# Layer 0's sums and layer 1's transposes moved from TensorE to VectorE and DRAM, and tiles of exponentials turned through DRAM with a fourth buffer

## The chip, the cores and the metric

The kernel runs on one NeuronCore of a Trainium2 chip. The metric is device time in microseconds of one execution. A profile is one more execution, recorded by the chip; in its rows PE is TensorE (PEld its weight loads), DVE is VectorE, ACT is ScalarE, POOL is GpSimd, SP is SyncE, which issues all DMAs here (SPq is its queue).

## The reference

Input x has 4 images of 128 channels by 64x64 pixels, so N = 4096 positions. In short:

```
# layer 0
g    = group_norm(x)                                    # 32 groups of channels
v,gt = split(sigmoid(conv_bn(g, Wvg)))                  # 1x1 convolutions
attn = softmax(q k^T / 8), q, k of 64 channels from g
x    = x + conv_bn(v attn^T * gt, Wp)
# layer 1, on tokens t = x^T, per image
h    = layer_norm(t)
q    = h W
t    = t + softmax(q q^T) h                             # q is also the key: symmetric
h2   = layer_norm(t)
wx   = batch_norm(h2 Wffn^T)                            # statistics over all tokens
y_i  = sigmoid(wx_i + y_(i-1) V^T)                      # recurrence along tokens
out  = (t + y)^T
```

All is float32. The softmax of a query divides the weighted sum of values by the sum of its exponentials. That sum (the denominator) and the transposes between "channels by positions" and "tokens by channels" are what the change is about.

## The kernel before, in words

`fast` (line 143) holds the whole of the work; `general` is another path that isn't run with these data. For each of four images (batches, b) `layer0` and then `layer1` are issued, both in blocks of 512 queries (n = 0..7). A block has four tiles of 128 positions (j). The remaining work of a block, once its attention is complete, is cut into small functions ("items") that are put in the list `pending`; the preparation of the next batch (norm, projections, gates) stands in the list `ahead`. The loops take one item from these lists at each step, so that their instructions stand between the big matmuls.

**Layer 0** (`attention`, line 178): 16 steps p per block. A step has two score matmuls (`ps`, line 200; 64 rows each, the two share the array), one exponential of 128x1024 on ScalarE (`e`, line 202), one VectorE add of the exponentials into `acc` (lines 207, 209), and, two steps later, four weighting matmuls into `o` (line 383). When a block is complete (`finish`, line 389) six items follow: `sums` (403) calls `denominators` (222), which adds the halves of `acc` and lets TensorE sum over the 128 partitions with four matmuls against a column of ones (`md`, line 227), and moves the input block `xb` to tokens; `projection` (407; `mt`, line 409) moves its result to tokens; `tokens` (412) adds the two and norms; `queries` (422; `mq`, line 424) makes `qt` of the moved layer norm `ht`.

**move** (line 235) is a transposition of 128x512 without TensorE: VectorE transposes 32x32 blocks into `d` (line 241), SP writes `d` to a DRAM tile `turn_d` (256 KB, line 244), waits for it, and reads it back in four parts in the other order (line 246).

**Layer 1** (`layer1`, line 435): since queries are keys, the scores are symmetric, and only the pairs of blocks (n, a) with a <= n are computed, in the order n = 6, 7, 5, ..., 0 and a = n, ..., 0. Each pair is two steps i. A step has two score matmuls (`ps`, line 562), two exponentials of 128x512 with their sums in `slots` (`e`, line 568), and two weighting matmuls later (`o`, line 455). For a < n VectorE also transposes the exponentials in blocks of 32x32 into `dd` (line 573, two buffers), and when a pair is complete 16 DMAs of 64 KB (line 594) carry `dd` to its turned place in `tt` (three buffers). Four steps later `reversed_products` (463) uses the turned tile for block a: four matmuls (`ot`, line 468), the sums of the tile into `slots` (line 473), and the sum of `ot` into `oacc` (`part`, lines 482 and 484).

A block n is complete after eight such parts; `finish` (495) loads its tokens `t` from DRAM and appends four items: `tokens` (504) sums the slots, transposes `oacc` on TensorE (`mt`, line 511), adds to the tokens (513) and norms into `h2`; `result` (520) transposes the tokens back on TensorE (`mr`, 523), copies them on ScalarE and stores them; `turn` (528) transposes `h2` on TensorE (`mh`, 531) and copies it to `th` on ScalarE (532); `inputs` (534) multiplies `th` (`mw`, 536) and stores the result for the recurrence. `layernorm` (250) works on VectorE, with two small instructions on GpSimd (lines 116, 117) in between.

The PSUM tiles `m` of all these items share one bank; the scores `ps` have two buffers, the exponentials `e` four. At the end the recurrence runs from line 640 on.

The instructions of an engine run in the order in which they stand in the built program. That is not quite the order of the code: when the program is built, an instruction is put where the builder expects its inputs to be ready, and later ones may go ahead of it. So `mw` may stand behind matmuls that the code has after it. SP's DMAs are one such order too.

Of the kernel before, what the change touches and what calls it, by code (L numbers as in the profile page):

```python
# [10 lines left out]
F32 = mybir.dt.float32  # L11
# [38 lines left out]
def conv_attn_hybrid_kernel(  # L50
# [14 lines left out]
    wxs_d = dram.tile([B, P, L // 2, G, 2], F32, name="wxs_d")  # L65
    t_d = dram.tile([B, NB, P, 4, NQ, 32], F32, name="t_d")

    turn_d = [dram.tile([P, 4, NQ, 32], F32, name=f"turn{i}_d") for i in range(8)]
    t2_d = dram.tile([B, C, N], F32, name="t2_d")
    wx_d = dram.tile([B, C, N], F32, name="wx_d")  # L70
# [43 lines left out]
    def inv_sqrt(dst, var, eps):  # L114
# [3 lines left out]

    par_ok = const.tile([P, 4], F32, name="par_ok")
    fast(  # L120
        tc, x, out, t_d, t2_d, wxs_d, turn_d,
        dict(qk=w[:, DQ : DQ + P], vs=w_vs, g=w_g, ps=w_ps, a=w_a, f=w_f, vt=v_t),
        col, par, par2, bpc, bc, ident, gavg, ones, shift, inv_sqrt, par_ok,
    )
# [16 lines left out]


def fast(
    tc, x, out, t_d, t2_d, wxs_d, turn_d, wt, col, par, par2, bpc, bc, ident, gavg, ones,
    shift, inv_sqrt, par_ok,
):
    nc = tc.nc
# [5 lines left out]
    with ExitStack() as st:  # L153
# [16 lines left out]

        done = set()

        def flush(until=None):

            while pending and until not in done:
                pending.popleft()()

        def attention(score_mm, bias, scale, weigh, finish, need):


            fifo: deque = deque()
            o = None

            def pop():
                nonlocal o
                n, p, e, acc = fifo.popleft()
                if p == 0:
                    o = None
                o = weigh(o, n, p, e)
                if p == PAIRS - 1:  # L190
                    finish(n, o, acc)

            for n in range(NB):
                acc = first = None
                for p in range(PAIRS):
                    need(n, p)
                    ps = ps_s.tile([P, 2, QB], F32, tag="s", name="ps")
                    for h in range(2):
                        lhsT, rhs = score_mm(n, p, h)
                        nc.tensor.matmul(ps[:, h, :], lhsT=lhsT, rhs=rhs, start=True, stop=True)  # L200
                    e = ep.tile([P, 2, QB], F32, tag="e", name="e")
                    nc.scalar.activation(e, ps, AF.Exp, scale=scale)  # L202
                    if p == 0:
                        first = e
                    elif p == 1:
                        acc = accp.tile([P, 2, QB], F32, tag="acc", name="acc", bufs=2)
                        nc.vector.tensor_tensor(acc, first, e, ALU.add)
                    else:
                        nc.vector.tensor_tensor(acc, acc, e, ALU.add)  # L209
                    fifo.append((n, p, e, acc))  # L210
                    if len(fifo) > LAG:
                        pop()
                        if p == 0:
                            pop()
                    if ahead:
                        ahead.popleft()()
                    elif pending and (p % 2 == 0 or len(pending) > 6):
                        pending.popleft()()
            while fifo:
                pop()  # L220

        def denominators(acc, at, rinv):

            nc.vector.tensor_tensor(acc[:, 0, :], acc[:, 0, :], acc[:, 1, :], ALU.add)
            m = ps_m.tile([P, NQ], F32, tag="m", name="md")
            for j in range(NQ):
                nc.tensor.matmul(  # L227
                    m[:, j : j + 1], lhsT=acc[:, 0, bass.ts(j, P)], rhs=ones,
                    start=True, stop=True,
                )  # L230
            den = den_all[:, at : at + NQ]
            nc.vector.tensor_copy(den, m)
            nc.vector.reciprocal(rinv, den)

        def move(blocks, dst):

            nonlocal n_moves
            d = work.tile([P, 4, NQ, 32], F32, tag="d", name="d", bufs=2)  # L240
            nc.vector.transpose(d.rearrange("q a j i -> q j a i"), blocks)
            via = turn_d[n_moves % len(turn_d)]
            n_moves += 1
            nc.sync.dma_start(via, d)
            for a in range(4):
                nc.sync.dma_start(dst[bass.ts(a, 32)], via[:, a].rearrange("(p i) j k -> i p j k", p=4))

        n_moves = 0

# [15 lines left out]
        def tiles(t):  # L265

            return [t[:, :, j, :] for j in range(NQ)]

        def quarters(t):
            return [t[:, j, :].rearrange("q (p i) -> q p i", p=4) for j in range(NQ)]  # L270
# [97 lines left out]
        def layer0(b, gate, q, k, v, need):  # L368
# [20 lines left out]
            def finish(n, o, acc):  # L389
# [10 lines left out]
                nc.sync.dma_start(xb, x[b, :, cs])  # L400
                nc.gpsimd.tensor_scalar(xb, xb, bpc, None, ALU.add)  # L401

                def sums():
                    denominators(acc, b * NT + n * NQ, rinv)
                    move(xb.rearrange("c (j f k) -> c j f k", j=NQ, f=4), t)

                def projection():
                    m = ps_m.tile([P, QB], F32, tag="m", name="mt")
                    nc.tensor.matmul(m, lhsT=wt["ps"], rhs=og, start=True, stop=True)  # L409
                    move(m.rearrange("c (j f k) -> c j f k", j=NQ, f=4), yt)  # L410

                def tokens():
                    for j in range(NQ):
                        nc.vector.scalar_tensor_tensor(
                            t[:, :, j, :], yt[:, :, j, :], rinv[:, j : j + 1], t[:, :, j, :],
                            ALU.mult, ALU.add,
                        )
# [17 lines left out]
        def layer1(b, h, qt):  # L435
# [6 lines left out]
            tt = big.tile([P, 3, NQ, NQ, NQ, 32], F32, tag="tt", name="tt")  # L442

            slots = accp.tile([P, NT, NB], F32, tag="slots", name="slots", bufs=2)
            fifo: deque = deque()
            turned: deque = deque()
            clock = 0
# [47 lines left out]
            def finish(n):  # L495
                cs = bass.ts(n, QB)
                rinv = stat.tile([P, NQ], F32, tag="rinv", name="rinv")
                t = work.tile([P, 4, NQ, 32], F32, tag="t", name="t1", bufs=2)
                h2 = work.tile([P, NQ, C], F32, tag="h2", name="h2")
                th = work.tile([P, QB], F32, tag="th", name="th")  # L500
                t1 = work.tile([P, NQ, C], F32, tag="og", name="t1b")
                nc.sync.dma_start(t, t_d[b, n])

                def tokens():
                    at = (B + b) * NT + n * NQ
                    den = den_all[:, at : at + NQ]
                    nc.vector.tensor_reduce(den, slots[:, bass.ts(n, NQ), :], AX.X, ALU.add)
                    nc.vector.reciprocal(rinv, den)
                    m = ps_m.tile([P, NQ, P], F32, tag="m", name="mt")
                    for j in range(NQ):  # L510
                        nc.tensor.transpose(m[:, j, :], oacc[:, n, bass.ts(j, P)], ident)
                    for j in range(NQ):
                        nc.vector.scalar_tensor_tensor(
                            t1[:, j, :].rearrange("q (p i) -> q p i", p=4),
                            m[:, j, :].rearrange("q (p i) -> q p i", p=4), rinv[:, j : j + 1],
                            t[:, :, j, :], ALU.mult, ALU.add,
                        )
                    layernorm(quarters(t1), quarters(h2))

                def result():  # L520
                    m = ps_m.tile([P, QB], F32, tag="m", name="mr")
                    for j in range(NQ):
                        nc.tensor.transpose(m[:, bass.ts(j, P)], t1[:, j, :], ident)
                    t2 = work.tile([P, QB], F32, tag="xb", name="t2")
                    nc.scalar.copy(t2, m)
                    nc.sync.dma_start(t2_d[b, :, cs], t2)

                def turn():
                    m = ps_m.tile([P, QB], F32, tag="m", name="mh")
                    for j in range(NQ):  # L530
                        nc.tensor.transpose(m[:, bass.ts(j, P)], h2[:, j, :], ident)  # L531
                    nc.scalar.copy(th, m)

                def inputs():
# [8 lines left out]
                        nc.vector.tensor_copy(wx, m)  # L543
                        nc.sync.dma_start(wxs_d[b, :, :, bass.ts(n, GB), :], wx)

                pending.extend([tokens, result, turn, inputs])


            for n in [NB - 2, NB - 1] + list(range(NB - 3, -1, -1)):
                o = None  # L550
                flush((b, n))
                for a in range(n, -1, -1):
                    if a < n:
                        d = dd[:, n_turned % 2]
                        t = tt[:, n_turned % 3]
                        n_turned += 1
                    for i in range(2):
                        ps = ps_s.tile([P, 2, QB], F32, tag="s", name="ps")
# [25 lines left out]
                                direct()  # L584
                        if turned and turned[0][0] <= clock:
                            reversed_products()
                        if pending:
                            pending.popleft()()
                        elif ahead:
                            ahead.popleft()()  # L590
                    if a < n:
                        for p in range(NQ):
                            for f in range(NQ):
                                nc.sync.dma_start(  # L594
                                    t[bass.ts(f, 32), p], d[bass.ts(p, 32), f]
                                )
                        turned.append((clock + 4, n, a, t))
            while fifo:
                direct()
            pending.extend([reversed_products] * len(turned))  # L600
# [529 lines left out]
```

## Time and profile before

| | us |
|---|---|
| three runs | 3160.39, 3161.45, 3161.61 (median 3161.45) |
| profiled execution | 3160.82 |
| its span | 3159.1 |
| TensorE busy | 3069.4 |
| VectorE busy | 1797.1 |
| ScalarE busy | 1125.2 |
| GpSimd busy | 140.6 |
| DMA | 242.17 MB, the queue's packets 27.5% of 16 engines' time |

The granted clock of TensorE over the span was 0.992. A group in the profile has its line, its engine and operation, what it writes and reads, the shape, the count, then busy time and the mean duration in ns, and behind the last bar the idle time of the engine just before the group's instructions and what ended it. A float32 matmul is two records of 512 columns. A matmul's end is modelled and overlaps the start of the next one, so the time from start to start says what one costs. A line of the order of time has the start, the duration, engine, line and count, and in brackets the wait ahead of it.

### The profile page before, as it was taken

The page shows a single profiled execution, that of the slowest core. Times are in us where ns is not written, and L with a number is a line of the kernel's source. Part 1 is how long each engine was busy: PE and PEld are TensorE (multiplying, and loading weights), DVE is VectorE, ACT ScalarE, POOL GpSimd, SP SyncE. Part 2 cuts the span into 40 slices and gives each one's busy share as a digit, 9 for nine tenths or more (in the row PEclk, how much of TensorE's full clock was granted, in tenths as well). Part 3 has the DMA queues.
Part 4 walks back from the last instruction along what each step waited for, and adds up shares of the span by engine and source line. Part 5 has one row for each costly group of instructions (what it writes and reads, how often), then busy time and mean ns, then how long its engine had stood idle before and what let it go on. Part 6 is the DMA issues. An engine that isn't in the chain of part 4 may idle for free.

```text
span 3159.1 us, 32271 instructions
## 1 busy us (share of the span) xinstructions
PE 3069.4 (97%) x10762; PEld 1374.7 (44%) x10762; DVE 1797.1 (57%) x2970; ACT 1125.2 (36%) x1978; POOL 140.6 (4%) x183
## 2 busy tenths in 40 slices
PE   7999999999999999999999999999999999999976
PEld 3444444444444444444444444444444444444433
DVE  6555556555555555555555555555555555455556
ACT  3433333333333333333333333333333333222324
POOL 0000000000000000000000000000000000000000
PEclk9999999999999999999999999999999999999988
DMA  1111133333111123333211113333321112543333
GB/s 50 34 47 54 54 95 93 91 91 92 51 50 54 54 64 94 94 92 93 74 51 54 54 37 102 92 94 92 91 55 54 54 41 66 146 102 90 99 117 156
DMA packets 233934, 242.17 MB, mean 77 GB/s; under 512 B 88736, under 2 KB 144544, under 8 KB 232736
## 3 DMA queue, kind: packets, MB, share of 16 engines
q1 hardware_dynamic: 233760, 240.02, 27.5%
q8 instruction: 88, 1.44, 0.2%
q14 instruction: 86, 0.70, 0.1%
HBM read 65.80 MB, written 56.62 MB: 39 GB/s over the span
## 4 chain that ended last, share of the span: by engine, by line
PE 89%; DVE 5%; SPq 2%; POOL 1%; DMA 1%; issue 1%; ACT 0%; DVEq 0%; ACTq 0%; POOLq 0%
PE o L383 28%; PE ps L200 15%; PE o L455 13%; PE ps L562 13%; PE ot L468 11%; SPq L594 2%; PE mt L409 1%; PE mw L536 1%; PE mq L424 1%; PE md L227 1%; PE pg L350 1%; PE pqk L315 1%; PE pv L335 1%; PE mh L531 1%; POOL rstd L117 1%
## 5 line engine op out<-in xcount | busy, mean ns | idle before, releaser
L383 PE MATMUL o<-e,nxt 64*128 64x512 f32 x4096 | 965.4, 589 | 0.0
L202 ACT ACTIVATE e<-ps 128x1024 f32<-128x1024 f32 x512 | 521.2, 1024 | 740.6 <-PE ps L200 734.4
L209 DVE TENSOR_TENSOR acc<-acc,e 128x1024 f32<-128x1024 f32 x448 | 546.4, 1220 | 386.7 <-ACT e L202 375.3
L568 ACT ACTIVATE e<-ps,shift 128x512 f32<-128x512 f32 x576 | 391.2, 684 | 772.8 <-PE ps L562 483.2
L383 PEld LDWEIGHTS o<-e,nxt 64*128 64x128 f32 x4096 | 399.5, 187 | 482.7 <-issue 474.6
L562 PE MATMUL ps<-qt 128*128 128x512 f32 x1152 | 546.7, 595 | 3.0 <-ACT e L568 3.0
L200 PE MATMUL ps<-nxt 64*128 64x512 f32 x2048 | 537.9, 603 | 0.3 <-ACT e L202 0.3
L455 PE MATMUL o<-e,h 128*128 128x512 f32 x1152 | 533.4, 592 | 0.0
L468 PE MATMUL ot<-tt,h 128*128 128x512 f32 x896 | 406.6, 597 | 3.6 <-DMA tt<-dd 3.5
L573 DVE STREAM_TRANSPOSE dd<-e 128x512 f32<-128x512 f32 x448 | 288.7, 685 | 109.0 <-ACT e L568 61.3
L455 PEld LDWEIGHTS o<-e,h 128*128 128x128 f32 x1152 | 216.9, 190 | 260.2 <-issue 259.0
L562 PEld LDWEIGHTS ps<-qt 128*128 128x128 f32 x1152 | 211.8, 191 | 243.2 <-issue 222.7
L200 PEld LDWEIGHTS ps<-nxt 64*128 64x128 f32 x2048 | 188.8, 187 | 245.4 <-issue 161.2
L468 PEld LDWEIGHTS ot<-tt,h 128*128 128x128 f32 x896 | 170.2, 191 | 218.2 <-issue 214.1
L473 DVE TENSOR_REDUCE slots<-tt 128x4 f32<-128x2048 f32 x112 | 252.8, 2258 | 8.6 <-DMA tt<-dd 8.2
L482 DVE TENSOR_TENSOR oacc<-oacc,ot 128x512 f32<-128x512 f32 x88 | 59.9, 681 | 209.2 <-PE ot L468 209.2
L116 POOL TENSOR_SCALAR rstd<-mv 128x4 f32<-128x4 f32 x64 | 14.5, 227 | 2518.9 <-DVE mv L257 2518.9
L568 ACT ACTIVATION_READ_ACCUMULATOR e<-ps,shift 128x1 f32 x576 | 113.1, 196 | 0.0
L401 POOL TENSOR_SCALAR xb<-xb,bpc 128x512 f32<-128x512 f32 x32 | 53.6, 1676 | 323.9 <-DMA xb<-in_x_dram 301.5
L117 POOL TENSOR_TENSOR rstd<-rstd,mhalf 128x4 f32<-128x4 f32 x64 | 66.4, 1037 | 5.3
L700 PE MATMUL ps_r<-y,w 128*128 128x256 f32 x168 | 53.0, 440 | 9.7 <-ACT y L697 6.2
L260 DVE TENSOR_SCALAR h<-t,mv,rstd 128x128 f32<-128x128 f32 x128 | 35.7, 343 | 45.2 <-POOL rstd L117 45.2
(113 smaller groups left out, 1411.8 us busy)
## 6 DMA issues: line engine op xcount, KB each, us to landing
tt<-dd SPq DMA_DIRECT2D x1792, 64.0 KB, 2.0
turn_d<-d SPq DMA_DIRECT2D x96, 256.0 KB, 2.0
t_d<-t SPq DMA_DIRECT2D x64, 256.0 KB, 2.0
nxt<-in_x_dram SPq DMA_DIRECT2D x16, 512.0 KB, 6.4
xb<-in_x_dram SPq DMA_DIRECT2D x32, 256.0 KB, 2.9
t<-turn_d SPq DMA_DIRECT2D x128, 64.0 KB, 2.0
yt<-turn_d SPq DMA_DIRECT2D x128, 64.0 KB, 2.0
ht<-turn_d SPq DMA_DIRECT2D x128, 64.0 KB, 2.0
```

What stands on the lines that cost most here:

```text
L117: nc.gpsimd.tensor_tensor(dst, dst, mhalf[:, :n], ALU.pow)
L200: nc.tensor.matmul(ps[:, h, :], lhsT=lhsT, rhs=rhs, start=True, stop=True)
L202: nc.scalar.activation(e, ps, AF.Exp, scale=scale)
L209: nc.vector.tensor_tensor(acc, acc, e, ALU.add)
L383: nc.tensor.matmul(o[r], lhsT=v[rs, p + h * PAIRS, :], rhs=e[rs, h, :], start=(p == 0 and h == 0), stop=(p == PAIRS - 1 and h == 1),)
L455: nc.tensor.matmul(o, lhsT=h[:, NQ * a + 2 * i + half, :], rhs=e[:, half, :], start=(a == n and i == 0 and half == 0), stop=(a == 0 and i ...
L468: nc.tensor.matmul(ot, lhsT=h[:, NQ * n + j, :], rhs=t[:, :, j, :, :].rearrange("q p k j -> q k p j"), start=(j == 0), stop=(j == NQ - 1),)
L473: nc.vector.tensor_reduce(slots[:, bass.ts(n, NQ), a], t.rearrange("q p b k j -> q b p (k j)"), AX.XY, ALU.add,)
L562: nc.tensor.matmul(ps[:, half, :], lhsT=qt[:, bass.ts(at, P)], rhs=qt[:, bass.ts(n, QB)], start=True, stop=True,)
L568: nc.scalar.activation(e[:, half, :], ps[:, half, :], AF.Exp, bias=shift, accum_out=slots[:, at, n : n + 1],)
L573: nc.vector.transpose(d.rearrange("q f b k j -> q k b f j")[:, 2 * i + half], e[:, half, :].rearrange("q (b f j) -> q b f j", b=NQ, f=NQ),)
L594: nc.sync.dma_start(t[bass.ts(f, 32), p], d[bass.ts(p, 32), f])
```

## The change

Layer 0's denominators are no longer summed by TensorE. VectorE transposes the added halves of `acc` in 32x32 blocks and sums each block's rows (`r`, 128x16); SP writes `r` to DRAM and reads it back in four small parts in the order of the tokens, and `tokens` adds up four partial sums. Both `acc` buffers become halves of one tile.

In layer 1, `oacc` goes to tokens by `move` (new item `weighted`), `h2` goes to `th` by `move`, and the result goes back by a transpose on VectorE and four DMAs to its place. `turn` and TensorE's transposes remain in blocks 0 and 1 of the last batch alone ("late"). A block's items become weighted, nothing, tokens, result, nothing, inputs, and an item of `ahead` is issued beside the ones named `light`. In block 0 of a layer 0 all that is pending is issued at step 15.

Turned tiles: `dd` is written to DRAM as a whole (1 MB) and read back in four parts, instead of 16 DMAs between buffers. They are used six steps later instead of four, and have a fourth buffer, `t4`, in the place that `acc` has in layer 0.

```diff
-        def denominators(acc, at, rinv):
+        def denominators(acc, at):
             nc.vector.tensor_tensor(acc[:, 0, :], acc[:, 0, :], acc[:, 1, :], ALU.add)
-            m = ps_m.tile([P, NQ], F32, tag="m", name="md")
-            for j in range(NQ):
-                nc.tensor.matmul(
-                    m[:, j : j + 1], lhsT=acc[:, 0, bass.ts(j, P)], rhs=ones,
-                    start=True, stop=True,
-                )
-            den = den_all[:, at : at + NQ]
-            nc.vector.tensor_copy(den, m)
-            nc.vector.reciprocal(rinv, den)
+            d = work.tile([P, 16, 32], F32, tag="d", name="dq", bufs=2)
+            nc.vector.transpose(d, acc[:, 0, :].rearrange("p (b k) -> p b k", k=32))
+            r = stat.tile([P, 16], F32, tag="r", name="r", bufs=2)
+            nc.vector.tensor_reduce(r, d, AX.X, ALU.add)
+            via = den_d[n_moves % len(den_d)]
+            rq = stat.tile([P, 4, NQ], F32, tag="rq", name="rq", bufs=2)
+            nc.sync.dma_start(via, r)
+            for f in range(4):
+                nc.sync.dma_start(
+                    rq[bass.ts(f, 32)],
+                    via[:, bass.ts(f, NQ)].rearrange("(p k) j -> k p j", p=4),
+                )
+            return rq
...
+                    if n == 0 and p == PAIRS - 1:
+                        flush()
...
                 def tokens():
+                    den = den_all[:, at : at + NQ]
+                    nc.vector.tensor_reduce(den, parts[0].rearrange("q p j -> q j p"), AX.X, ALU.add)
+                    nc.vector.reciprocal(rinv, den)
...
+                late = b == B - 1 and n < 2
+                def weighted():
                     at = (B + b) * NT + n * NQ
                     den = den_all[:, at : at + NQ]
                     nc.vector.tensor_reduce(den, slots[:, bass.ts(n, NQ), :], AX.X, ALU.add)
                     nc.vector.reciprocal(rinv, den)
-                    m = ps_m.tile([P, NQ, P], F32, tag="m", name="mt")
-                    for j in range(NQ):
-                        nc.tensor.transpose(m[:, j, :], oacc[:, n, bass.ts(j, P)], ident)
+                    if not late:
+                        move(oacc[:, n, :].rearrange("c (j f k) -> c j f k", j=NQ, f=4), ot, nc.sync)
+                def tokens():
...
+                    layernorm(tiles(t), quarters(h2))
+                    if not late:
+                        move(
+                            h2.rearrange("q j (p i) -> q j p i", p=4),
+                            th.rearrange("c (f j k) -> c f j k", f=4, j=NQ), nc.sync,
+                        )
                 def result():
-                    m = ps_m.tile([P, QB], F32, tag="m", name="mr")
-                    for j in range(NQ):
-                        nc.tensor.transpose(m[:, bass.ts(j, P)], t1[:, j, :], ident)
-                    t2 = work.tile([P, QB], F32, tag="xb", name="t2")
-                    nc.scalar.copy(t2, m)
-                    nc.sync.dma_start(t2_d[b, :, cs], t2)
+                    d = work.tile([P, 4, NQ, 32], F32, tag="d", name="d", bufs=2)
+                    nc.vector.transpose(
+                        d.rearrange("q p j k -> q j p k"), t.rearrange("q p j i -> q j p i")
+                    )
+                    to = t2_d[b, :, cs].rearrange("(p i) (f r) -> f i p r", p=4, f=4)
+                    for f in range(4):
+                        nc.sync.dma_start(
+                            to[f], d[bass.ts(f, 32)].rearrange("i p j k -> i p (j k)")
+                        )
...
-                pending.extend([tokens, result, turn, inputs])
+                if late:
+                    pending.extend([weighted, tokens, turn, inputs, result])
+                else:
+                    light.update([weighted, tokens, result])
+                    pending.extend([weighted, nothing, tokens, result, nothing, inputs])
...
-                        t = tt[:, n_turned % 3]
+                        t = tt[:, n_turned % 4 - 1] if n_turned % 4 else fourth()
...
-                        if pending:
-                            pending.popleft()()
-                        elif ahead:
+                        item = pending.popleft() if pending else nothing
+                        item()
+                        if item in light and ahead:
                             ahead.popleft()()
                     if a < n:
-                        for p in range(NQ):
-                            for f in range(NQ):
-                                nc.sync.dma_start(
-                                    t[bass.ts(f, 32), p], d[bass.ts(p, 32), f]
-                                )
-                        turned.append((clock + 4, n, a, t))
+                        via = tiles_d[n_turned % len(tiles_d)]
+                        nc.sync.dma_start(via, d)
+                        for f in range(NQ):
+                            nc.sync.dma_start(
+                                t[bass.ts(f, 32)], via[:, f].rearrange("(p i) b k j -> i p b k j", p=4)
+                            )
+                        turned.append((clock + 6, n, a, t))
```

## The prediction

> **What bounds the kernel now.** I read the page's busy shares first, then the chain that ended last, then the groups of TensorE by shape, and last the order of time around single steps.
>
> ```profile
> PE 3069.4 (97%) x10762; PEld 1374.7 (44%) x10762; DVE 1797.1 (57%) x2970; ACT 1125.2 (36%) x1978; POOL 140.6 (4%) x183
> ...
> PE 89%; DVE 5%; SPq 2%; POOL 1%; DMA 1%; issue 1%; ACT 0%; DVEq 0%; ACTq 0%; POOLq 0%
> ```
>
> TensorE is busy 97% of the span and 89% of the chain; VectorE has 43% to spare. Work taken off TensorE shortens the run, and anything that makes TensorE wait lengthens it by as much. Four groups of TensorE are what the change is about:
>
> ```profile
> L424 PE MATMUL mq<-ht,w 128*128 128x512 f32 x64 | 35.7, 639 | 0.6 <-DMA ht<-turn_d 0.6
> ...
> L227 PE MATMUL md<-ones,acc 128*128 128x1 f32 x256 | 33.3, 251 | 0.0
> L531 PE MATMUL mh<-ident,h 128*128 128x128 f32 x128 | 28.3, 305 | 17.6 <-DVE h L260 14.8 <-ACT e L568 2.8
> L511 PE MATMUL mt<-ident,oacc 128*128 128x128 f32 x128 | 20.0, 278 | 2.5 <-DVE wxs L540 1.4 <-DVE oacc L482 1.1
> L523 PE MATMUL mr<-ident,t1b 128*128 128x128 f32 x128 | 19.6, 276 | 1.3 <-DVE t1b L513 1.3
> ```
>
> After the bar stands TensorE's idle time ahead of the group: hardly any, except 17.6 us ahead of `mh`, which waits for the layer norm. The first line is the one place where TensorE already uses a tile that was moved through DRAM (`ht`), and there it waits 0.6 us in all.
>
> **What goes.** Busy times of small matmuls overlap, so I take the time from each matmul's start to the next one's, summed over the trace: `md` 30.8, `mt` 16.8, `mr` 17.5, `mh` 23.0 us. `md` and `mr` go wholly, `mt` and `mh` in 30 of 32 blocks: 30.8 + 15.8 + 17.5 + 21.6 = 85.7 us. The wait ahead of `mh` goes with it, 17.6 x 30/32 = 16.5. Together **-102 us**, all on the path.
>
> **What is hidden.** VectorE gets two instructions more per block in layer 0 (a transpose, 0.70 as `d<-xb`, and a sum over 128x512, between 0.16 and 2.26 by the rows of the two TENSOR_REDUCE shapes; I take 0.7) and three transposes in layer 1: about 32 x 1.4 + 92 x 0.7 = 109 us, 61% of the span; ScalarE loses 37 us of copies. Neither is the bound. In layer 0 the sums' moves stand on SP's queue ahead of `yt`: four more issues, 1.8 us. `ht` was ready about 2.8 us before `mq` (reads issued from 1008.04 to 1009.85, 2.0 to landing, `mq` at 1014.65), so this is covered; uncovered it would be 28 x 1 us. The sums' pieces of 16 bytes have no row; the nearest are 0.5 to 4 KB (2.9 to 3.2 us to landing) and 64 KB (2.0): nobody waits for them before `yt`.
>
> A tile of exponentials now costs SP 16 issues (11.7 us at 603.95). It becomes one write of 1 MB and four reads. The write lies between 2.0 (256 KB) and 14.7 us (2 MB, four at once); I take 5, nearer to 512 KB (6.4). With 1.8 of issues and 3 to land the trip is 10 us. In the order of the built program a tile's use stands 20 to 48 us of TensorE time behind its last transpose, so it is covered. SP holds some back behind a move: the write of tile (7,2), ready 25 us earlier, stands behind block 6's `move(h2)`, and has 3 us left by this count. If the cover fails, the price is that of the second rival below.
>
> **What is added: waits of TensorE for `th`.** `mw` (line 536) used `th` straight from TensorE and ScalarE. Now `th` comes from `move(h2)`. The trip and the work before it, in layer 0 of the profile:
>
> ```profile
> 993.96 0.72 DVE L241 STREAM_TRANSPOSE d<-mt 128x512 f32<-128x512 f32 x1
> 994.70 0.34 SPq L244 DMA_DIRECT2D turn_d<-d  x1
> 996.72 1.74 SPq L246 DMA_DIRECT2D yt<-turn_d  x4
> 1000.27 1.14 DVE L414 SCALAR_TENSOR_TENSOR t<-yt,rinv,t 128x128 f32<-128x128 f32 x4 [0.39 <-DMA yt<-turn_d]
> ...
> 1005.15 0.71 DVE L241 STREAM_TRANSPOSE d<-h 128x512 f32<-128x512 f32 x1
> ```
>
> The transpose ends at 994.68, VectorE waits for the moved tile until 1000.27: a **trip of 5.6 us**. From the first of `tokens` (1000.27) to the transpose of its result (1005.15) it takes 4.9, and 0.7 for that transpose. In the built order of the changed program `mw` doesn't stand that far back. Block 6 of batch 0: behind the `ot` of tile (7,5) TensorE has one score call, the four of the next `ot`, four score calls, four of another `ot`, one score call, then `mw`: 14 calls of two passes of 0.429 us (four passes start 1.72 apart), 12.0 us from the end of that first `ot`. VectorE, from the same end: 0.2, sum into `oacc` 0.68, slots 2.25, four transposes 2.7, `oacc` 0.68, then 4.9 + 0.7: 12.1. So TensorE stands at `mw` when the move only begins: late by 12.1 + 5.6 - 12.0 = 5.7 us. The same sum (VectorE's stretch + 5.6 - TensorE's stretch, from one common end) for the other blocks of a batch:
>
> - 7: 1.6 + 5.6 - 4.3 = 2.9
> - 5: 13.5 + 5.6 - 15.4 = 3.7
> - 4: in time, by 7
> - 3: 11.0 + 5.6 - 9.4 = 7.2 (from the second score of the next layer 0)
> - 2: 11.9 + 5.6 - 9.9 = 7.6 (in layer 0, from its step 5)
> - 0: W's move first, 1.6 + 5.6, then 4.9 + 0.7 + 5.6, against 12.9: 5.5
> - 1: ot lands 5.2 behind the start of block 0's `mw`, then 5.6 + 5.6, against 8.2: 8.2
>
> (blocks 2, 0, 1 finish in the next batch's layer 0; behind the forced flush `mw` of 0 and 1 are 7 us apart.) That is 40.8 us a batch, 122 in three. In the last batch, without the next one's projections: 5.7 + 2.9 + 2.0 + 3.4 = 14. At the end, before: 18.4 us from the last `ot` to the last `mw`. After: `th` of block 2 lands 9.7 behind that `ot`, `mw` 0.9, VectorE's two reads of it 1.6, then blocks 0 and 1 as before, 17.1: 29.3, or +11. In blocks 6, 7 and 5 SP issues a tile's 1 MB between the move's write and its reads: 0 to 2.9 us each (1 MB at the 358 GB/s with which the results left); I take 1, 12 in all. **Waits: 122 + 14 + 11 + 12 = +159 us.**
>
> What is queued behind a waiting `mw` is everything: TensorE takes its instructions in order, ScalarE has two score buffers, VectorE the four exponentials.
>
> **And the clock.** A wait costs more than itself:
>
> ```profile
> 2741.34 3.60 PE L562 MATMUL ps<-qt 128*128 128x512 f32 x8
> 2747.96 6.63 PE L468 MATMUL ot<-tt,h 128*128 128x512 f32 x8 [3.02 <-DMA tt<-dd]
> 2754.43 2.74 PE L562 MATMUL ps<-qt 128*128 128x512 f32 x6
> ```
>
> After 3.02 us of idling eight matmuls took 6.47 us instead of 3.43: 3.0 lost. Some 18 of the waits above are over 3.4 us (five a batch in three, three at the end). Each costs between 0 and 3.4 (two clock windows at half speed, partly in the wait); I take 2: **+36**.
>
> The Trainium skill ("TensorE: Matmul & The Clock Gate", "What's actually happening") says that the clock halves after an idle window of about 3.4 us and needs a busy one to come back. The row had it after 3.02. By the page's rule the waits of 2 to 3 us cost no clock; by the row they might, six more at 2, +12.
>
> **Sum.** 3160.8 (the profiled execution: span 3159.1 and 1.7 around it; the median of the runs is 3161.45) - 102 + 159 + 36 = **3254 us**.
>
> **Rivals.**
>
> 1. *The cover holds.* The waits are differences of two stretches of 8 to 15 us. If `th` comes 5 us earlier at each place than I count (VectorE's stretch begins earlier, because TensorE is held up ahead of it by the score buffers, or the built order is nearer to the chip than I read it), 1 + 0 + 0 + 2 + 3 + 0.5 + 3 = 9.5 a batch are left, 5 in the last, 11 at the end, no clock: -102 + 45 = -57, **3104**. It is decided at 102 us of waits and clock: 26 waits of 3.9. For it: `mq` has waited 0.6 us in all for the same kind of move, and `mt`, `mr`, `mh` were placed so that TensorE hardly waits. Against it: the places of `mq` are 8.8 us behind its transpose, those of `mw` 0 to 8. With no wait at all: 3059.
> 2. *The tiles are late.* SP gives a tile's write, its reads and the moves in one order, each held by the one before. If the trip of 10 us passes the 20 to 48 us of cover, TensorE waits for `tt` as it did for 3.5 us. At 3 us for a quarter of 112 tiles, on top of my forecast: +84, **3338**.
> 3. *Waits cost their time alone*, no clock, no tile in the way: 3160.8 - 102 + 147 = **3206**.
> 4. That the small matmuls stay is excluded: the built order has no `md` or `mr`, and `mt` and `mh` in two blocks.
>
> **How the numbers follow.** Forecast, 3254, with rival 3 as its lower part: 0.70, own range 3190 to 3320. Rival 1 down to no wait: 0.20 (3059 to 3154). Rival 2: 0.06 (over 3320). The rest, 0.04, within 0.2%, some 6 us, which is about what a measurement can tell from no change. Faster 0.20, same 0.04, slower 0.76. From 3110 to 3320 holds the forecast, no change and the upper half of rival 1: 0.70 + 0.04 + 0.08.
>
> **What would show it.** Right: no rows of `md` and `mr`, 8 records each of `mt` and `mh`; a new wait PE `mw` <- DMA `th<-turn_d`, about 26 times, 150 us in all, longest in the first 25 us of layers 0; half-clock stretches after it; PE's share down to about 92%; PE `ot` <- DMA `tt` still a few us; dd's writes no longer wait 47 us for `tt<-dd`. Wrong, if TensorE's idle time ahead of `mw` is under 60 us: then the built order or VectorE's stretch was misread. If TensorE waits for `tt`, the tile's trip was.

## The result and the profile after

The changed kernel takes **3454.35 us** (median of 4 runs, 3452.39 to 3457.24) against 3161.53 in the same comparison: ratio 1.0928, interval 1.0911 to 1.0944. The forecast was slower, 3254, range to 3320; the loss is 293 us where 93 were forecast. From here line numbers of the changed kernel are those of its own profile: 431 is `mt`, 585 `mw`, 615 layer 1's scores, 621 its exponentials, 626 the transposes into `dd`, 412 and 413 `og`, 436 the last sum of the denominators.

First the page of the changed kernel, busy shares and the chain that ended last:

```profile
PE 3114.7 (90%) x10138; PEld 1352.2 (39%) x10138; DVE 1893.4 (55%) x3126; ACT 1088.6 (32%) x1916; POOL 137.6 (4%) x183
...
PE 70%; DVE 11%; DMA 10%; SPq 3%; issue 2%; ACT 2%; POOL 1%; DVEq 0%; ACTq 0%
```

TensorE has 624 matmuls fewer, and its part of the chain falls from 89% to 70%: VectorE and DMA now hold it up. Who waits for whom is in the view of waits (engine, line, what is waited for: total us, times, longest):

```profile
ACT e L621 <- DVE dd L626: 306.8, 43, 13.9
...
DVE den_all L436 <- DMA rq<-den_d: 145.6, 29, 6.4
...
PE mw L585 <- DMA th<-turn_d: 79.9, 18, 7.0
...
PE ps L615 <- ACT e L621: 69.9, 26, 6.4
PE mt L431 <- DVE og L413: 69.4, 28, 3.7
...
DVE dd L626 <- DMA tiles_d<-dd: 30.3, 16, 10.0
...
PE ot L501 <- DMA tt<-tiles_d: 14.4, 7, 5.7
```

Before the change ScalarE waited far less for the transposes of `dd`, and TensorE never waited at layer 0's `mt`:

```profile
ACT e L568 <- DVE dd L573: 48.0, 14, 7.6
```

TensorE's waits at `mw` were forecast. Those at `mt`, in layer 0, and at layer 1's scores were not, and they are nearly as large. The one at `mt` is read in the order of time, a block of layer 0 in the second batch:

```profile
1023.85 0.64 DVE L239 TENSOR_REDUCE r<-dq 128x16 f32<-128x512 f32 x1
...
1024.52 0.34 SPq L242 DMA_DIRECT2D den_d<-r  x1
...
1026.45 1.80 SPq L244 DMA_DIRECT2D rq<-den_d  x4
...
1029.54 0.18 DVE L436 TENSOR_REDUCE den_all<-rq 128x4 f32<-128x16 f32 x1 [5.05 <-DMA rq<-den_d]
1029.76 0.18 DVE L437 RECIPROCAL rinv<-den_all 128x4 f32<-128x4 f32 x1
1029.85 0.66 DVE L412 TENSOR_TENSOR og<-o,og 128x512 f32<-128x512 f32 x1
1030.55 0.69 DVE L413 TENSOR_TENSOR og<-og,nxt 128x512 f32<-128x512 f32 x1
...
1031.30 1.55 PE L431 MATMUL mt<-og,w 128*128 128x512 f32 x2 [2.32 <-DVE og L413]
```

`den_all` isn't needed before `tokens`, but the builder has put it into VectorE's queue ahead of `og`. VectorE stands 5.05 us for the denominators' trip, `og` behind it is late, and TensorE stands 2.32 us at `mt`. The same stretch by windows, with the granted clock in the column behind POOL's:

```profile
1022.00:1031.00 9.00, 6.97 (x34) 2.85 (x30) 3.85 (x8) 3.55 (x4) 1.58 (x1) 1.00 0.33 89
1031.00:1038.00 7.00, 6.71 (x22) 2.66 (x24) 4.45 (x5) 1.27 (x2) 0.00 (x0) 0.76 0.14 48
```

In the seven microseconds behind that wait the mean clock is 0.76: one record of 3.41 us at half speed. A half-speed record begins so behind 23 of the 28 waits at `mt`.

To size the parts I sum TensorE's time from each matmul's start to the next one's, beyond 0.43 us (a full matmul at full clock), up to the scan; matmuls that take longer only because the clock is halved are kept apart. In us:

| kernel | `mt`, layer 0 | `mw` | scores, layer 1 | all waits | half clock |
|---|---|---|---|---|---|
| before | 0 | 0 | 4 | 39 | 4 |
| after | 75 | 81 | 76 | 312 | 102 |

The figures move by a few us with the length from which a stop is called a wait. 371 more, less the 85.7 of matmuls that went, is 285 of the 293. The order of time agrees: the scan's first matmul starts at 3334.3 us, at 3050.1 before, 284 later. The rest lies behind that start, where the last blocks finish (33.3 us from the start of the last `ot` to that of the last `mw`, 18.8 before).

### The profile page after: what moved, and what is told of

Same layout as the page of the kernel before. It is cut to its first block, busy times and chain, and to the rows that moved or that the text cites. A ratio compares the mean times of both kernels' runs of the same rounds, so it can differ in the third digit from the quotient of the medians.

```text
span 3455.4 us, 30391 instructions
## 1 busy us (share of the span) xinstructions
PE 3114.7 (90%) x10138; PEld 1352.2 (39%) x10138; DVE 1893.4 (55%) x3126; ACT 1088.6 (32%) x1916; POOL 137.6 (4%) x183
## 4 chain that ended last, share of the span: by engine, by line
PE 70%; DVE 11%; DMA 10%; SPq 3%; issue 2%; ACT 2%; POOL 1%; DVEq 0%; ACTq 0%
PE o L402 19%; PE o L488 13%; PE ps L615 13%; PE ps L206 11%; PE ot L501 8%; DMA turn_d<-d 3%; DMA tiles_d<-dd 2%; DMA rq<-den_d 1%; DVE dd L626 1%; PE mt L431 1%; DVE acc L215 1%; SPq L261 1%; PE mw L585 1%; PE pv L354 1%; DMA tt<-tiles_d 1%
## 5 line engine op out<-in xcount | busy, mean ns | idle before, releaser
L402 PE MATMUL o<-e,nxt 64*128 64x512 f32 x4096 | 1013.6, 600 | 0.0
L402 PEld LDWEIGHTS o<-e,nxt 64*128 64x128 f32 x4096 | 422.0, 193 | 514.5 <-issue 506.4
L206 PE MATMUL ps<-nxt 64*128 64x512 f32 x2048 | 586.7, 624 | 1.2 <-ACT e L208 1.2
L501 PE MATMUL ot<-tt,h 128*128 128x512 f32 x672 | 318.2, 622 | 14.4 <-DMA tt<-tiles_d 14.4
L501 PEld LDWEIGHTS ot<-tt,h 128*128 128x128 f32 x672 | 133.6, 201 | 188.7 <-issue 181.9
L506 DVE TENSOR_REDUCE slots<-tt 128x4 f32<-128x2048 f32 x84 | 190.7, 2270 | 7.7 <-DMA tt<-tiles_d 7.6
L585 PE MATMUL mw<-th,w 128*128 128x512 f32 x64 | 54.7, 951 | 81.3 <-DMA th<-turn_d 79.9
L275 DVE TENSOR_SCALAR h<-t,mv,rstd 128x128 f32<-128x128 f32 x256 | 71.4, 343 | 92.1 <-POOL rstd L119 92.1
L431 PE MATMUL mt<-og,w 128*128 128x512 f32 x64 | 41.9, 741 | 69.4 <-DVE og L413 69.4
L501 PE MATMUL ot<-t,h 128*128 128x512 f32 x224 | 100.7, 592 | 0.0
```

Source lines behind the costliest of these rows:

```text
L402: nc.tensor.matmul(o[r], lhsT=v[rs, p + h * PAIRS, :], rhs=e[rs, h, :], start=(p == 0 and h == 0), stop=(p == PAIRS - 1 and h == 1),)
L501: nc.tensor.matmul(ot, lhsT=h[:, NQ * n + j, :], rhs=t[:, :, j, :, :].rearrange("q p k j -> q k p j"), start=(j == 0), stop=(j == NQ - 1),)
L506: nc.vector.tensor_reduce(slots[:, bass.ts(n, NQ), a], t.rearrange("q p b k j -> q b p (k j)"), AX.XY, ALU.add,)
L585: nc.tensor.matmul(m, lhsT=wt["f"], rhs=th, start=True, stop=True)
```

## The experiments

Each was run beside the kernel before (3160 to 3162). The parts are called sums (layer 0), moves (layer 1's transposes with the new order of pending items), tiles (write and reads in DRAM), and steps (fourth buffer, six steps, the forced `flush` in block 0). In e1, e3 and e4 part of the old order of a block's tokens is kept (in e1 and e4 for the tokens, not for the denominators; in e3 for layer 0, not for layer 1), so they compute other numbers with the same instructions. All other kernels compute the whole reference.

**The parts alone.** e1, the kernel before with the sums:

```diff
-                nc.tensor.matmul(m[:, j : j + 1], lhsT=acc[:, 0, bass.ts(j, P)], rhs=ones, ...)
+            nc.vector.transpose(d, acc[:, 0, :].rearrange("p (b k) -> p b k", k=32))
+            nc.vector.tensor_reduce(r, d, AX.X, ALU.add)
+            nc.sync.dma_start(via, r)      # and four reads into rq
...
+                    nc.vector.tensor_reduce(den, rq..., AX.X, ALU.add)   # in tokens()
```

> The kernel before with the change's layer 0 alone (denominators by VectorE and DRAM). Theory Q (VectorE waits 5 us in its queue for `rq`, `og` stands behind it, TensorE waits for `og` at `mt`): from the changed kernel's layer 0, -31 (md) + 66 (32 waits at `mt`) + 11 (first scores) + 30 to 45 of half clock = about +80, 3240 (3215 to 3270); `mt` <- VectorE `og` in some 28 of 32 blocks. Rival M (the loss is all of layer 1's moves and tiles, the sums' trip is hidden as the prediction said): -31, 3131.

Measured: 3245.37, 1.0269 (1.0251 to 1.0286). The waits of this kernel:

```profile
DVE den_all L424 <- DMA rq<-den_d: 164.0, 32, 6.7
...
PE mt L419 <- DVE og L401: 72.0, 28, 4.0
```

Theory Q, in size and place: 28 waits at `mt`, none of them there before. e4 is the same with the last sum on GpSimd:

```diff
-                    nc.vector.tensor_reduce(den, parts[0]..., AX.X, ALU.add)
-                    nc.vector.reciprocal(rinv, den)
+                    nc.gpsimd.tensor_tensor(rq[:, 0], rq[:, 0], rq[:, 1], ALU.add)
+                    nc.gpsimd.tensor_tensor(rq[:, 2], rq[:, 2], rq[:, 3], ALU.add)
+                    nc.gpsimd.tensor_tensor(den, rq[:, 0], rq[:, 2], ALU.add)
+                    nc.gpsimd.tensor_tensor(rinv, den, minus1, ALU.pow)
```

> As the sums alone, but the last sum of `rq` and its reciprocal are done by GpSimd (three additions and a power of -1), so that VectorE has the same added transpose and sum and the same transfers stand on SP, but nothing in VectorE's queue waits for `rq`. Theory Q: no waits at `mt`, -31: 3131 (3120 to 3145). Rival V (VectorE's added work, or SP's four more issues, make `og` or `mq` late): as the sums alone, or 28 x 1 us more at `mq`.

Measured: 3136.70, 0.9926 (0.9909 to 0.9942). No wait at `mt` is left. VectorE does the same transpose and sum, so it was the wait in its queue and not the work. Of the 31 us of `md`, 24 arrive; TensorE waits 7.3 at `mq` for `ht` instead, in the last block of each batch. SP has four more issues there, but that they are the cause was not tried.

e2, the tiles with the steps; e5, the tiles alone; e6, the steps alone:

```diff
# e2 and e5: one write of 1 MB and four reads for 16 transfers
-                        for p in range(NQ):
...
+                        via = tiles_d[n_turned % len(tiles_d)]
+                        nc.sync.dma_start(via, d)
...
# e2 and e6, with the fourth buffer and the flush
-                        turned.append((clock + 4, n, a, t))
+                        turned.append((clock + 6, n, a, t))
```

> The kernel before with the tiles of exponentials by way of DRAM alone, fourth buffer and six steps. Theory Q: the tiles themselves cost next to nothing, 3150 to 3180; VectorE's transposes no longer wait for `tt<-dd`. Rival T (the two buffers of `dd` are held by the write of 1 MB, 5.9 us to landing; VectorE, ScalarE and then the scores wait): the scores' 72 us of waits and some 30 to 40 of half clock come here, 3250 or more.

> The kernel before with tiles through DRAM alone (one write of 1 MB, four reads), but its three buffers and four steps. The tiles with fourth buffer and six steps cost +96 without TensorE waiting for a tile. Theory O (with the write and the reads in DRAM the builder sets VectorE's and TensorE's instructions in another order, in which exponentials' transposes and projections stand in bunches): the same order of cost, +60 to +120, 3220 to 3280, waits of TensorE for exponentials, gates and values, not for `tt`. Rival S (the six steps, the fourth buffer and the flush do it): 3150 to 3170. Rival C (cover of four steps is too short for the longer trip): 3280 or more with waits at `ot` for `tt`.

> The kernel before with the fourth buffer, the flush and the use six steps later, but a tile's 16 transfers from buffer to buffer as before. Theory O: no bunches, 3145 to 3165. Rival S (steps, buffer or flush): about 3256, as with the tiles through DRAM.

Measured: e2 3256.24, 1.0315 (1.0290 to 1.0340); e5 3179.42, 1.0056 (1.0040 to 1.0073); e6 3171.42, 1.0031 (1.0019 to 1.0044). So +96 together, +18 and +10 alone: neither O nor S as I put them, it takes both. My first theory (tiles cost nothing) fell. In e2 TensorE hardly waits for a tile; its waits are at layer 1's scores (34), gates `pg` (19) and values (14), 18 more at half clock. Rival T's mechanism isn't seen either: VectorE waits for `dd`'s write once, 7.1 us. ScalarE's longest wait for `dd`'s transposes is 14.0 us, 7.6 before: they stand late in VectorE's queue.

e3, the moves alone, with the 16 transfers and four steps of before.

> The kernel before with layer 1's transposes by VectorE and moves alone, with the change's order of the pending items; tiles by the 16 transfers as before. Removed from TensorE: 15.8 + 17.5 + 21.6 and the 16.5 ahead of `mh`, 71. Theory Q, waits at `mw` 87 and half clock about 40 from them, the scores' waits 72 with their clock because the moves and the packed items delay VectorE: +87 +40 +72 +20 -71 = about +150, 3310. Rival T (scores' waits belong to the tiles): +87 +40 -71 = +56, 3218. If the sums were all of it: -71, 3090.

Measured: 3181.90, 1.0064 (1.0047 to 1.0081). Only +22: `mw` waits 21, `ot` 25, the values `pv` 22, half clock 26. All three numbers missed; the moves are cheap while tiles go from buffer to buffer.

**From the changed kernel back.** e7 puts the last sum on GpSimd, e8 puts the 16 transfers back, e12 is e7 with `clock + 4`, e9 is e12 without fourth buffer and flush, e13 is e9 with the 16 transfers.

> The changed kernel, with the last sum of the denominators and the reciprocal on GpSimd, as in the run that cost 24 us less than the kernel before. Theory Q: the waits at `mt` and their half clock go as they did alone, -109: 3345 (3325 to 3370). Rival: VectorE is late anyway in the changed kernel, and `mt`'s waits become waits at other places (first scores, `mq`): less than half of it, 3400 or more.

> The changed kernel with a tile's 16 transfers in place of the way through DRAM (fourth buffer and six steps kept). The parts alone cost +85, +96 and +22; all three +293, 90 more than their sum. If those 90 come of tiles and moves together (the bunched order puts `mw` right behind the transpose whose move it needs): -96 -90, 3268 (3240 to 3290), and `mw` waits about as long as with the moves alone (18 us by DMA `th`). If they come of sums and moves together: -96, 3358.

> The changed kernel with the last sum on GpSimd and the use four steps later, but with fourth buffer and flush. Theory F1 (the forced flush issues the last blocks' items one right behind another, so that `mw` has nothing between it and its move): the 67 us of waits at `mw` in layer 0 stay, the scores' 75 go: 3250 (3225 to 3275). Theory F2 (six steps alone): as with three buffers and no flush.

> The changed kernel with the last sum on GpSimd (3348), and besides with three buffers, the use four steps later and no forced flush in block 0 of layer 0; moves and tiles through DRAM stay. Alone, the parts gave -24 (sums with GpSimd), +22 (moves), +18 (tiles through DRAM at four steps). Theory F (the fourth buffer with six steps and its flush is what makes moves and tiles dear): their sum, 3178 (3160 to 3215). Rival X (moves and tiles through DRAM hurt each other whatever the steps): 3280 or more.

> The kernel of 3251 (sums with GpSimd, moves, tiles through DRAM, three buffers, four steps) with the tiles' 16 transfers as before, so sums with GpSimd and moves are left. Alone these gave -24 and +22. Theory X (moves and tiles through DRAM hurt each other): 3158 (3145 to 3185). Rival Y (sums' transfers and moves hurt each other on VectorE and SP, tiles cost their 18): 3233 (3215 or more).

| kernel | us | ratio, interval | step |
|---|---|---|---|
| after | 3454.35 | 1.0928 (1.0911 to 1.0944) | |
| e7: last sum off VectorE's queue | 3348.13 | 1.0591 (1.0574 to 1.0609) | -106 |
| e12: and four steps for six | 3282.52 | 1.0378 (1.0361 to 1.0396) | -66 |
| e9: and no fourth buffer, no flush | 3251.20 | 1.0290 (1.0273 to 1.0307) | -31 |
| e13: and 16 transfers for DRAM | 3156.53 | 0.9984 (0.9974 to 0.9993) | -95 |
| e8: after, only the 16 transfers | 3391.31 | 1.0724 (1.0706 to 1.0742) | -63 from after |

e7 came out as expected (3345), and so did e13 (3158): theory X. e9 and e12 missed both their numbers. e8 too: with the steps and VectorE's wait kept, TensorE waits 101 us at `mw` and 79 at `mt`, not less than in the changed kernel. The steps therefore depend on the order in which parts are undone; the chain of four adds up from 3156.53 to 3454.35.

What is it in e9 that e13 doesn't have? TensorE's waits at the scores, 47 us against none, and at the next batch's projections `pqk`, 24 against 2. In e9's order of time:

```profile
649.33 1.88 PE L608 MATMUL ps<-qt 128*128 128x512 f32 x4
...
654.76 3.60 PE L494 MATMUL ot<-tt,h 128*128 128x512 f32 x8
...
655.25 2.28 DVE L499 TENSOR_REDUCE slots<-tt 128x4 f32<-128x2048 f32 x1
...
658.39 0.69 DVE L508 TENSOR_TENSOR oacc<-oacc,ot 128x512 f32<-128x512 f32 x1 [0.86 <-PE ot L494]
659.00 4.92 DVE L619 STREAM_TRANSPOSE dd<-e 128x512 f32<-128x512 f32 x8
660.39 0.69 ACT L614 ACTIVATE e<-ps,shift 128x512 f32<-128x512 f32 x1 [5.51 <-DVE dd L619]
...
661.89 3.05 PE L608 MATMUL ps<-qt 128*128 128x512 f32 x4 [3.54 <-ACT e L614]
```

Eight transposes run back to back from 659.00, behind a sum over `ot` for which VectorE had even stood 0.86 us; the last exponentials ahead of them were written by 650. ScalarE has no free buffer until then and stands 5.51 us, TensorE has two score banks and stands 3.54. In the built order of this kernel two tiles' `ot` stand back to back at 17 places of a run; with the 16 transfers at none. (The stretch above is not one of them. The tiles alone, e5, have 14 such places and cost 18 us, so this order is at most dear beside the moves.) I tried three ways to move that:

e14 issues the next batch's projections only beside empty items (`light` holds `nothing` alone); e16 issues layer 1's moves by GpSimd (`queue=nc.gpsimd`); e17 issues the tiles' transfers by ScalarE (`nc.scalar.dma_start`). All start from e9, 3251.

> The kernel of 3251 with the next batch's projections issued only beside the empty items, not beside `weighted`, `tokens` and `result`. Theory L (a projection in the same step as a layer norm loads VectorE's queue, and projections wait for each other's copies): the 24 us at `pqk` and some 10 of the scores' go, with clock, 3215 (3195 to 3230). Rival: the waits at `pqk` move to the steps where the projections then stand; within 10 us of 3251.

> The kernel of 3251 with layer 1's two moves issued by GpSimd instead of SP. On SP the move of `oacc` is issued 10.6 us (median of 30) behind its transpose, since SP waits there for a tile's transposes and for its write to land. Theory P (SP's one order for tiles and moves is what makes them dear together): the moves go at once, `mw` and VectorE's `otk` hardly wait, 3180 (3165 to 3205). Theory O (the order in which the builder sets VectorE's instructions when tiles go through DRAM: exponentials' transposes behind sums of `ot`): the order is as bunched as before, 3235 or more.

> The kernel of 3251 with a tile's write and reads issued by ScalarE instead of SP. The built order then has no double `ot` (17 pairs of tiles' products back to back before, none now). Theory O: the waits of the scores (46) and of tiles (29) go with their clock, 3150 to 3190. Rival A (ScalarE stands while a write of 1 MB lands, 6 us 112 times, and the exponentials behind it): 3300 or more.

Measured: e14 3242.31, 1.0260 (1.0233 to 1.0287), the rival: the packed projections aren't it. e16 3362.74, 1.0639 (1.0621 to 1.0657). Two waits of e9, and the same two in e16:

```profile
PE ps L608 <- ACT e L614: 42.2, 16, 3.5
PE mw L578 <- DMA th<-turn_d: 32.3, 8, 5.6
```

```profile
PE mw L578 <- DMA th<-turn_d: 183.4, 27, 11.6
...
PE ps L608 <- ACT e L614: 14.5, 8, 2.7
```

The waits at `ot` went from 29 to 3, those at the scores fell to 14.5 though all 17 double `ot` stayed, but a move issued by GpSimd is late at `mw`, where TensorE waits more than five times as long as in e9. e17 3344.23, 1.0577 (1.0560 to 1.0595):

```profile
PE mw L578 <- DMA th<-turn_d: 69.7, 13, 13.8
PE mq L450 <- DMA ht<-turn_d: 49.9, 4, 14.8
PE mw L578 <- DMA tt<-tiles_d: 45.5, 8, 7.2
PE ps L608 <- ACT e L614: 31.7, 8, 7.4
```

No double `ot` is left, and the scores still wait 32 us. So the double `ot` alone are not what makes the scores wait. The number is rival A's, and ScalarE does stand for transfers ahead of its exponentials; but most of TensorE's wait is at `mw` and `mq`, which use moved blocks, and not at the scores. Why those moves are late there I did not look into. Both gave a new wait larger than the one they took away, so **what makes tiles and moves dear together (95 us) stays open**. That VectorE's transposes then stand late in its queue is seen; why the builder puts them there is not, and no kernel here has the tiles in DRAM with the old order.

e10, from e7: `h2` turned by TensorE again, without its move.

> The changed kernel with the last sum on GpSimd (3348), and layer 1's `h2` turned by TensorE and copied by ScalarE again, without its move through DRAM. Theory: the 89 us of waits at `mw` go with some 30 of half clock, `mh` (22) and 10 of waits ahead of it come back: 3260 (3240 to 3285). Rival V (VectorE's queue is late at the batch's end, so `mh` waits for the layer norm instead, or the scores for exponentials): 3310 or more.

Measured: 3305.35, 1.0461 (1.0444 to 1.0479). Half of what I expected, and the rival's wait: 67 us at `mh`, most of it for the layer norm's `h2`. The wait has changed its name: VectorE is late there. It waits 11.6 us for the move of `oacc`; the rest of its lateness I did not take apart.

**What is worth keeping.** e11, the kernel before with e4's sums and the result by VectorE and four transfers; e15, with `oacc` moved as well and the result issued behind `turn` and `inputs`.

> The kernel before with the sums as in the run that took 3137 (GpSimd for the last sum), and of layer 1's changes only the result: `t` turned by VectorE and written by four transfers, no `mr` on TensorE and no copy on ScalarE. Nobody on the chip waits for that result before the end. Theory: 3137 - 17.5 = 3119 (3105 to 3128). Rival V (VectorE's added transpose comes ahead of the exponentials' in its queue, or its four transfers ahead of a move on SP): 3137 or more.

> The kernel of 3129 (sums with GpSimd, result by VectorE), and besides `oacc` turned by VectorE and moved through DRAM instead of by TensorE (30 of 32 blocks). If nothing waits for that move: -16, 3113. Rival (VectorE waits in its queue for `otk`, 20 us in 7 places with the moves alone, and exponentials' transposes stand behind): 3135 or more.

Measured: e11 **3129.35**, 0.9899 (0.9883 to 0.9916), faster than both kernels, though only 7 of the 17.5 us of `mr` arrive. e15 3169.82, 1.0025 (1.0015 to 1.0036): the rival's number, but not its wait. VectorE hardly waits for `otk`; TensorE waits at `mh`, 32 us from start to start, and 24 us more go at half clock:

```profile
PE mh L564 <- DVE h L269: 37.9, 9, 5.3
...
DVE t L544 <- DMA otk<-turn_d: 3.0, 3, 1.1
```

The result has no reader on the chip before the end; `oacc` has one, behind a trip. But in e15 `turn` also stands right behind `tokens`, without `result` between them, and that alone could make `mh` wait for the layer norm. The two were not separated.

## Why the prediction was wrong

The sign was right; the size fails at three steps.

1. *"nobody waits for them before `yt`"*, the denominators' trip at nothing. **This is the largest single miss: 106 us** (e7), 109 between e1 and e4. The data isn't needed earlier, but the instruction that waits for it stands ahead of the last instruction of `og` in VectorE's queue in 29 of 32 blocks, and TensorE waits at `mt` in 28. Only in the first block of the second, third and fourth batch does it stand behind `og`. The fallback price, "28 x 1 us", was for SP's four issues; e4 has 7.3 us at `mq`, in four blocks.
2. *"so it is covered"*, the tiles through DRAM. The cover held: TensorE waits 14.4 us for `tt`. What I didn't weigh is that other transfers and steps make the builder set VectorE's and TensorE's instructions in another order. Steps, flush and tiles beside the moves cost 66 + 31 + 95 = 192 us on the way back, where 12 were forecast for tiles in the way. That the order changes is seen (17 double `ot`, none before; ScalarE waits 306.8 us for `dd`, 48.0 before). How the order makes the 192 us is not shown and stays open.
3. *The clock*, 18 windows at 2 us. The size of one was right: 102 us of half clock in 56 records, 1.8 each. The number wasn't, because waits under 3 us count.

Right was the work removed (the rows of `md` and `mr` are gone, `mt` and `mh` are in two blocks) and the mechanism of `mw`, at half its size: 81 us against 159. At the first of the batches' boundaries the three long waits are 7.2, 6.7 and 5.9 us where 7.6, 5.5 and 8.2 were forecast. Elsewhere they are shorter than forecast: in the first batch 0.4 for blocks 6 and 7 (5.7 and 2.9 forecast) and 1.9 for block 3 (7.2). Ahead of blocks 6 and 7 the scores' waits had already held TensorE up: by 6.4 us until 607.5, with `mw` at 609.3, and by 5.9 until 692.4, with `mw` at 694.3. The end, +11 by forecast, is +14.5. TensorE's share was to be 92% and is 90%. Rival 1 named its condition rightly (TensorE held up ahead by the score buffers), but that holding-up costs the same time. Rival 2 (tiles late) didn't happen. Neither of the signs of being wrong that the prediction named came up (`mw` has 81 us, not under 60; `tt` has 14.4): most of the loss lay at places for which it had named none.

## What to carry to other kernels

A transfer's latency is hidden only if no instruction that waits for it stands ahead of other work in an in-order queue: look up that instruction's neighbours in the steady state, in every block. Put such a last step on an engine with nothing urgent behind it, and move to the slower path first what nobody reads back (e11; that e15 lost by the trip itself is not shown). Where a scheduler sets the order, changing how data travels changes the order too, so measure the parts alone and together: tiles and steps, +18 and +10 alone, became 96 together and 192 beside the moves.

## What the runs showed of the hardware

Waits of 2 to 3 us can halve TensorE's clock. By length of wait (start to start beyond 0.43 us, before the scan), the changed kernel has a half-speed record beginning in or within 3.5 us behind none of 20 waits of 0.7 to 1.5 us, 3 of 13 of 1.5 to 2, 12 of 18 of 2 to 2.5, and 21 of 21 of 2.5 to 3. The length alone doesn't decide it: in e1 it is 11 of 13 waits of 2.5 to 3 us, in e9 5 of 9. The records are mostly of 3.41 us or a multiple. The Trainium skill ("TensorE: Matmul & The Clock Gate", "What's actually happening") has windows of that length, running freely, and lets the clock fall after one idle window of about 3.4 us. The length agrees; the threshold doesn't: in the changed kernel 33 of 39 waits of 2 to 3 us were enough. By the page's rule nearly all waits at `mt` (2.2 to 2.9 us, three of 3.8) would have cost no clock; but e1 has 24 half-speed records before the scan, 92 us in all, and e4, without those waits, three, 14 us.

A write of 1 MB to DRAM landed 5.9 us behind its issue, a read of a quarter of it 6.3 to 6.7, a moved block's write of 256 KB 2.0 by SP and 3.3 by GpSimd (e16).
